# Layer 2's int8 feed-forward: whole numbers in bfloat16, scales at the result, bias and sum by GpSimd

## The chip, the cores and the metric

One core of a Trainium2 chip runs the whole program. The metric is the time of one execution on the device in microseconds, as the median of a few runs. Five engines work side by side, each in the order of its own queue: TensorE (PE in the profile, its weight loads PEld), VectorE (DVE), ScalarE (ACT), GpSimd (POOL) and SyncE (SP), which only issues transfers here. They hand work to each other through semaphores. [...]

## The reference, cut to what matters

A stream `x` of 4 x 256 tokens with 256 features goes through four layers. Each layer adds an attention and a feed-forward to the stream, both of the normalised stream and both under a gate, a tanh of one number:

```python
x = x + jnp.tanh(g_xattn[1]) * _L1_xattn_ref(_layernorm(x, axis=-1), ctx_512, ...)
x = x + jnp.tanh(g_ffn[1])   * _L1_ffn_ref(_layernorm(x, axis=-1), ...)      # ternary weights
x = x + jnp.tanh(g_xattn[2]) * _L2_xattn_ref(_layernorm(x, axis=-1), ctx_512, ...)
x = x + jnp.tanh(g_ffn[2])   * _L2_ffn_ref(_layernorm(x, axis=-1), ...)      # the changed stage
x = x + jnp.tanh(g_xattn[3]) * _L3_xattn_ref(...)
```

Layers 0 and 3 have a mixture of experts as feed-forward, layer 1 a two-layer network with ternary weights, layer 2 one matrix, quantised to 8 bits together with its input:

```python
def _L2_ffn_ref(x, weight, bias):
    w_max = jnp.clip(jnp.max(jnp.abs(weight), axis=1, keepdims=True), 1e-08, None)
    w_scale = w_max / 127
    w_q = jnp.clip(jnp.round(weight / w_scale), -128, 127).astype(jnp.int8)
    x_max = jnp.max(jnp.abs(x), axis=2, keepdims=True)
    x_scale = jnp.maximum(x_max / 127, 1e-12)
    x_q = jnp.clip(jnp.round(x / x_scale), -128, 127).astype(jnp.int8)
    acc = jnp.einsum('bnd,od->bno', x_q.astype(jnp.int32), w_q.astype(jnp.int32))
    y = acc.astype(jnp.float32) * x_scale * w_scale[None, None, :]
    return y + bias
```

`weight` is 256 x 256; each of its rows has a scale, and so has each token.

## The kernel before, in words

The tokens are cut into eight tiles of 128, `x[0]` to `x[7]`, which stay in SBUF all the time; four tiles make a group `g` of 512 tokens. The stages run one after the other: attention 0, the experts of layer 0, attention 1, layer 1's feed-forward, attention 2, the changed feed-forward (`ffn2`), attention 3, the experts of layer 3. The kernel is written as a dataflow, and a planner lays out each engine's queue at compile time: it goes through the program with a model of the durations, and when an engine is free it takes the earliest instruction of the program whose inputs are there. An instruction can thus be placed far ahead of its neighbours in the program, unless an edge holds it (`behind(later, sooner)`: not sooner than) or its tile has no buffer: tiles of one tag share a fixed number of buffers (`t4` six, `xn` six, `hits` one, the PSUM tag `mm` four).

Layer 2's weights are in the program in `weights2`, called ahead of layer 1's feed-forward. The weight lies as two halves `c` of 128 output rows. L1687 to L1690 find the scale `ws` of each row and its reciprocal; an edge keeps them behind attention 1's normalisation (`kept["normal"]`). L1695 to L1697 round (by adding and subtracting the constant ROUND), clip and multiply with the scale again, into a tile `wq` of the tag `t4`; L1698 multiplies with the gate. Four float32 transposes (L1704) and a copy by ScalarE (L1707) give `wqT`; the bias is one row of 1 KB (L1709), multiplied with the gate (L1710).

Around that time VectorE also makes layer 1's ternary weights (`ternary1`, L1608 and L1609, eight times each), and `ffn1` begins with transposes L1629 of its input's first group, which ScalarE and VectorE split into three bfloat16 terms (L1631 to L1634), for the products L1649 and the gelu L1656; L1665 is its second product, in bfloat16 with 256 columns.

In the changed stage, `rounded(g)` normalises a group (`layernorm`: statistics L382 and L383, root L385, reciprocal L386, shift L390, the normalised tiles L394 by ScalarE into four tiles of the tag `xn`), finds each token's largest value (L1719), and rounds by L1723 and L1724, the second of which multiplies with the token's scale again. Group 0's rounding is already called in attention 2. `ffn2` transposes the tiles in float32 (L409) into `xT` (one copy by ScalarE, L140, one by VectorE, L142); then for each tile TensorE lays down the bias (L1735, a product of one row of ones with one row of bias), adds two products (L1737), and VectorE adds the result to `x[t]` (L1740). Attention 3 begins with the normalisation of group 0 and its queries (L424).

Other lines that are spoken of: L440 is GpSimd's multiplication of the attention weights of one tile, L438 and L439 the sums and reciprocals ahead of it, L459 the addition of an attention's result to `x[t]`, L659 and L986 an attention's last products. L686 (VectorE) and L694, L695 (GpSimd) are attention 0's rotation of the queries. In layer 0's expert blocks GpSimd issues for each of 55 blocks a gather of its tokens (L1206) and a scatter of its result (L1305); at the end the sums are loaded back and added (L1488). L1320 and L1323 are VectorE's preparation of the last three blocks. L1602 and L1603 are two small steps of the ternary weights, L1030 and L871 memsets that belong to later stages.

Of the kernel before, what the change touches and what calls it, by code (L numbers as in the profile page):

```python
# [30 lines left out]
F32 = mybir.dt.float32  # L31
# [8 lines left out]
P = 128  # L40
# [48 lines left out]
def tile_flamingo(ctx: ExitStack, tc: tile.TileContext, a: dict, out: bass.AP):  # L89
# [1301 lines left out]
    def ffn0(gate):  # L1391
# [112 lines left out]
        )  # L1504
        moe.run(SURE0, collect)
        kept["fold1"] = ended[0]
        load_experts3(0, EARLY3, added[-1])

    def ffn3(gate):
# [169 lines left out]
        load_experts3(EARLY3, E3)  # L1679


    def weights2(gate):

        w = loaded["L2"][:, 1536:2048].rearrange("p (c d) -> p c d", c=2)
        ws = small([P, 2], "ws", 1)
        inv = small([P, 2], "wsi", 1)
        largest = nc.vector.tensor_reduce(ws, w, AX.X, ALU.max, apply_absolute_value=True)  # L1687
        behind(largest, kept["normal"])
        nc.vector.tensor_scalar(ws, ws, 1e-8, 1.0 / 127.0, ALU.max, ALU.mult)
        nc.vector.reciprocal(inv, ws)  # L1690
        wq = t4([P, 2, D], "wq")
        for c in range(2):

            q = wq[:, c, :]
            nc.vector.tensor_scalar(q, w[:, c, :], inv[:, c : c + 1], ROUND, ALU.mult, ALU.add)  # L1695
            nc.vector.tensor_scalar(q, q, ROUND, 127.0, ALU.subtract, ALU.min)
            nc.vector.tensor_scalar(q, q, -128.0, ws[:, c : c + 1], ALU.max, ALU.mult)  # L1697
        nc.vector.tensor_scalar(wq, wq, gate, None, ALU.mult)  # L1698
        kept_2 = sb.tile([P, 768], F32, tag="hits", name="kept_2", bufs=1)
        wqT = kept_2[:, :512].rearrange("p (d o) -> p d o", d=2)  # L1700
        ps = ps_mm()
        for d in range(2):
            for c in range(2):
                nc.tensor.transpose(  # L1704
                    ps[:, d * D + c * P : d * D + (c + 1) * P], wq[:, c, d * P : (d + 1) * P], ident
                )
        nc.scalar.copy(wqT.rearrange("p d o -> p (d o)"), ps)  # L1707
        bias_2 = kept_2[:1, 512:]
        nc.sync.dma_start(out=bias_2, in_=a["L2_bias"].partition_broadcast(1))  # L1709
        nc.vector.tensor_scalar(bias_2, bias_2, gate[:1], None, ALU.mult)  # L1710
        return wqT, bias_2

    def rounded(g):

        xn = layernorm(g, True)
        xs = small([P, TPG], "xs")
        xi = small([P, TPG], "xi")
        for i, n in enumerate(xn):
            nc.vector.tensor_reduce(xs[:, i : i + 1], n, AX.X, ALU.max, apply_absolute_value=True)  # L1719
        nc.vector.tensor_scalar(xs, xs, 1.0 / 127.0, 1e-12, ALU.mult, ALU.max)  # L1720
        nc.vector.reciprocal(xi, xs)
        for i, n in enumerate(xn):
            nc.vector.tensor_scalar(n, n, xi[:, i : i + 1], ROUND, ALU.mult, ALU.add)  # L1723
            nc.vector.tensor_scalar(n, n, ROUND, xs[:, i : i + 1], ALU.subtract, ALU.mult)  # L1724
        return xn

    def ffn2(gate):
        used("L2")
        wqT, bias_2 = kept.pop("weights2")
        for g in range(NG):  # L1730
            xqT = transposed(kept.pop("rounded") if g == 0 else rounded(g))
            for i in range(TPG):
                t = g * TPG + i
                ps = ps_mm()
                nc.tensor.matmul(ps[:, :D], ones[:1], bias_2, start=True, stop=False)  # L1735
                for d in range(2):
                    nc.tensor.matmul(  # L1737
                        ps[:, :D], xqT[:, d, i * P : (i + 1) * P], wqT[:, d, :], start=False, stop=(d == 1)
                    )
                nc.vector.tensor_tensor(x[t], ps[:, :D], x[t], ALU.add)  # L1740

    steps = [
        attention0,
# [159 lines left out]
```

## Time and profile before

| | |
|---|---|
| median of 3 runs | 934.46 us (933.23 to 937.22) |
| the profiled execution | 937.0 us, of which the span from first to last instruction 934.9 |
| TensorE busy | 850.5 us, 91% of the span |
| VectorE busy | 515.8 us, 55% |
| GpSimd busy | 317.9 us, 34% |
| ScalarE busy | 286.1 us, 31% |
| mean granted TensorE clock | 0.963 |
| attention 1 and ternary weights | 457 to 564 us |
| layer 1's feed-forward | 564 to 612 us |
| attention 2 | 612 to 677 us |
| the changed stage | 677 to 700 us |

A group in the profile is named by line, engine, operation, tile written from tile read, and shape; "idle before" is how long its engine stood still ahead of it and what ended that. The chain that ended last is followed back from the program's last instruction, at each step to what released it; what isn't on it has slack. A line of the chain in order of time gives the start, the duration and the engine, tile and line. TensorE takes a float32 product in two passes that are recorded one by one, so a float32 matmul counts twice among its instructions.

### The profile page before, as it was taken

What the parts mean: (1) busy time and instruction counts of PE and PEld (TensorE: products, weight loads), DVE (VectorE), ACT (ScalarE), POOL (GpSimd) and SP (SyncE); (2) the same over time, 40 slices, a digit from 0 to 9 for tenths busy, and PEclk for the clock granted to TensorE, in tenths of its full rate; (3) what the DMA queues carried; (4) which work ended last, traced back from release to release, by engine and by line L of the source; (5) the groups of instructions that cost most, each with busy time, mean ns of one, the idle gap of its engine ahead of it and who ended that gap; (6) DMA issues with size and microseconds to landing.
All of it is one profiled execution on the core that took longest, in us unless ns stands there. A gap on an engine that the chain in (4) does not pass through costs nothing.

```text
span 934.9 us, 12575 instructions
## 1 busy us (share of the span) xinstructions
PE 850.5 (91%) x4395; PEld 544.5 (58%) x4395; DVE 515.8 (55%) x1319; ACT 286.1 (31%) x545; POOL 317.9 (34%) x248
## 2 busy tenths in 40 slices
PE   5999998999978999899599978999889899999993
PEld 3544335875746777576446864755555556566662
DVE  3667446755843435333466787968767864222220
ACT  1221103434212332223133428526535531122220
POOL 0445442320027888887102220003202402244321
PEclk8999999999989999999899999989889999999997
DMA  9410218101684554555740000450000012122222
GB/s 343 139 35 6 96 48 270 48 23 28 215 248 82 87 87 80 85 83 80 219 159 1 1 1 1 143 200 1 1 23 1 1 47 64 46 47 46 35 23 63
DMA packets 38481, 74.90 MB, mean 80 GB/s; under 512 B 6225, under 2 KB 26290, under 8 KB 37042
## 3 DMA queue, kind: packets, MB, share of 16 engines
q1 hardware_dynamic: 24050, 53.34, 16.7%
q0 software_dynamic: 14016, 19.94, 13.4%
q8 instruction: 39, 0.64, 0.3%
q10 hardware_dynamic: 352, 0.79, 0.2%
q14 instruction: 24, 0.20, 0.1%
HBM read 58.87 MB, written 16.22 MB: 80 GB/s over the span
## 4 chain that ended last, share of the span: by engine, by line
PE 74%; DVE 9%; DMA 8%; ACT 4%; issue 2%; POOL 2%; SPq 0%; another core or an unknown queue 0%; POOLq 0%; ACTq 0%; DVEq 0%
PE wide L424 14%; PE wide L1264 8%; PE mm L1290 7%; PE wide L1253 6%; PE mm L424 5%; PE mm L659 4%; DMA xs<-xd,big 2%; PE wide L644 2%; PE mm L1665 2%; PE mm L454 2%; PE mm L1649 2%; PE mm L1280 2%; DMA sums<-ring,big 2%; PE wide L944 2%; PE mm L709 2%
## 5 line engine op out<-in xcount | busy, mean ns | idle before, releaser
L440 POOL TENSOR_TENSOR attn<-attn,sm 128x1024 f32<-128x1024 f32 x32 | 60.8, 1901 | 281.9 <-DVE sm L439 228.5
L1273 DVE SCALAR_TENSOR_TENSOR blk<-wide,blk 128x176 f32<-128x176 f32 (+1 forms) x75 | 37.0, 494 | 148.0 <-ACT blk L1272 141.0
L424 PE MATMUL wide<-xT,big 128*128 128x512 f32 (+1 forms) x240 | 111.3, 611 | 0.3 <-ACT xT L140 0.2
L1305 POOL DMA_INDIRECT sums<-ring,big x52 | 82.7, 1590 | 18.7 <-issue 7.8
L686 DVE TENSOR_TENSOR rope<-wide,big 128x512 f32<-128x512 f32 x96 | 59.6, 684 | 50.1 <-PE wide L424 50.1
L1253 PE MATMUL wide<-big,blk 128*128 x220 | 79.2, 478 | 3.3 <-issue 1.6
L1206 POOL DMA_INDIRECT xs<-xd,big x55 | 56.1, 1019 | 67.0 <-PE mm L581 43.1
L424 PEld LDWEIGHTS wide<-xT,big 128*128 128x128 f32 (+1 forms) x240 | 44.1, 192 | 57.1 <-issue 49.8
L1264 PE MATMUL wide<-big,blk 128*128 x160 | 74.3, 606 | 2.6 <-DMA sums<-x 2.2
L1272 ACT ACTIVATE blk<-wide 128x176 f32<-128x176 f32 (+1 forms) x75 | 29.4, 392 | 137.5 <-PE wide L1264 69.0
L1290 PE MATMUL mm<-big,blk 88*128 x220 | 58.2, 385 | 2.8 <-ACT blk L1282 2.1
L659 PE MATMUL mm<-vo,attnT 128*128 128x256 f32 x256 | 58.6, 382 | 1.5 <-ACT attnT L455 1.5
L1290 PEld LDWEIGHTS mm<-big,blk 88*128 88x128 f32 x220 | 42.0, 193 | 19.4 <-ACT blk L1282 3.8
L659 PEld LDWEIGHTS mm<-vo,attnT 128*128 128x128 f32 x256 | 47.4, 190 | 9.0 <-ACT attnT L455 3.2
L1253 PEld LDWEIGHTS wide<-big,blk 128*128 128x128 f32 x220 | 40.6, 197 | 18.6 <-issue 6.1
L455 ACT COPY attnT<-mm 128x512 f32<-128x512 f32 x64 | 34.6, 588 | 53.6 <-PE mm L454 53.2
L1264 PEld LDWEIGHTS wide<-big,blk 128*128 128x128 f32 x160 | 29.3, 194 | 33.3 <-issue 33.3
L438 DVE TENSOR_REDUCE sm<-attn 128x16 f32<-128x1024 f32 x32 | 38.9, 1215 | 16.2 <-ACT attn L432 13.7
L1305 POOL DMA_INDIRECT sums<-ring,scratch x20 | 31.5, 1573 | 41.0 <-ACT ring L1301 17.0
L1206 POOL DMA_INDIRECT xs<-xd,scratch x20 | 19.4, 972 | 73.5 <-PE mm L1218 49.7
L1219 DVE COPY blk<-mm 128x256 f32<-128x256 f32 x75 | 31.4, 419 | 17.0 <-PE mm L1218 14.4
L454 PE MATMUL mm<-ident,attn 128*128 128x128 f32 x256 | 35.1, 282 | 6.2 <-POOL attn L440 6.1
(311 smaller groups left out, 1607.2 us busy)
## 6 DMA issues: line engine op xcount, KB each, us to landing
big<-in_L_w_gate_up SPq DMA_DIRECT2D x8, 1024.0 KB, 8.9
big<-in_L_w SPq DMA_DIRECT2D x3, 1408.0 KB, 8.1
big<-in_L_w_down SPq DMA_DIRECT2D x8, 512.0 KB, 6.1
w_L_qk<-in_L_qk SPq DMA_DIRECT2D x4, 896.0 KB
big<-in_L_w SPq DMA_DIRECT2D x3, 768.0 KB, 7.1
big<-in_L_wo SPq DMA_DIRECT2D x1, 2048.0 KB, 13.0
xd<-xn SPq DMA_DIRECT2D x16, 128.0 KB, 1.8
w_L_wq<-in_L_wq SPq DMA_DIRECT2D x2, 1024.0 KB, 4.8
```

What stands on the lines that cost most here:

```text
L424: nc.tensor.matmul(ps, w(c), xT[:, c, :], start=(c == 0), stop=(c == 1))
L438: nc.vector.tensor_reduce(sm, e, AX.X, ALU.add)
L440: nc.gpsimd.tensor_tensor(e, e, sm.unsqueeze(2).to_broadcast([P, groups, n]), ALU.mult)
L454: nc.tensor.transpose(ps[:, i * P : (i + 1) * P], ev[:, pr * P : (pr + 1) * P], ident)
L659: nc.tensor.matmul(ps[:, :D], aT[:, s, :], vo[:, s, :], start=(s == 0), stop=(s == NP - 1))
L686: nc.vector.tensor_tensor(m[:, s, :].rearrange("q (b t) -> q b t", t=S), ps[:, s, :].rearrange("q (b t) -> q b t", t=S), table, ALU.mult,)
L1206: nc.gpsimd.indirect_dma_start(out=xs, out_offset=None, in_=self.xd, in_offset=bass.IndirectOffsetOnAxis(ap=self.gather[:, b : b + 1].bitc ...
L1253: nc.tensor.matmul(ps[:, 0, : 2 * n], st[:, c * P : (c + 1) * P], self.w[:, bass.ds(r + c * 2 * n, 2 * n)], start=False, stop=(c == 1),)
L1264: nc.tensor.matmul(ps[:, k, :n], st[:, c * P : (c + 1) * P], self.w[:, bass.ds(r + (2 * c + k) * n, n)], start=(c == 0), stop=(c == 1),)
L1273: self.weighted = nc.vector.scalar_tensor_tensor(s, lin, self.weight.pop(b), s, ALU.mult, ALU.mult)
L1290: nc.tensor.matmul(ps[:, :D], hT[:k, j * P : (j + 1) * P], self.w[:k, bass.ds(r + j * D, D)], start=(j == 0), stop=(j == self.n - 1),)
L1305: nc.gpsimd.indirect_dma_start(out=self.sums[b % len(self.sums)], out_offset=bass.IndirectOffsetOnAxis(ap=self.scatter[:, b : b + 1].bitca ...
```

## The change

The weights' quantisation is taken out of `weights2` into a new function `quantised`, which is called at the end of `ffn0`, with no edge to anything. It rounds and clips in place in the loaded weights, and leaves the whole numbers as bfloat16 in the first half of each 128 words; the scale isn't multiplied in. `weights2` transposes them in bfloat16, loads the bias into all 128 partitions and has GpSimd multiply it with the gate; it also makes a tile `scale`, each column's weight scale times the gate, in all partitions, by a product of ones with the scales on a diagonal (`spread`).

`rounded` no longer multiplies with the token's scale; its second step writes bfloat16 in place. GpSimd adds the bias to the group's `x[t]` there. `ffn2` transposes in bfloat16, has both copies made by ScalarE, and multiplies bfloat16 by bfloat16 with two products for a tile and none for the bias. VectorE then takes the result out of PSUM, times the token's scale and the column's scale, into a tile `y` of the tag `xn`, and GpSimd adds `y` to `x[t]`.

```diff
@@ -1504,6 +1504,7 @@
         )
         moe.run(SURE0, collect)
         kept["fold1"] = ended[0]
+        kept["quantised"] = quantised()
         load_experts3(0, EARLY3, added[-1])
 
     def ffn3(gate):
@@ -1679,39 +1680,48 @@
         load_experts3(EARLY3, E3)
 
 
-    def weights2(gate):
+    def quantised():
 
         w = loaded["L2"][:, 1536:2048].rearrange("p (c d) -> p c d", c=2)
+        q16 = loaded["L2"][:, 1536:2048].bitcast(BF16).rearrange("p (c d q) -> p c d q", c=2, d=2)[:, :, :, :P]
         ws = small([P, 2], "ws", 1)
         inv = small([P, 2], "wsi", 1)
-        largest = nc.vector.tensor_reduce(ws, w, AX.X, ALU.max, apply_absolute_value=True)
-        behind(largest, kept["normal"])
+        nc.vector.tensor_reduce(ws, w, AX.X, ALU.max, apply_absolute_value=True)
         nc.vector.tensor_scalar(ws, ws, 1e-8, 1.0 / 127.0, ALU.max, ALU.mult)
         nc.vector.reciprocal(inv, ws)
-        wq = t4([P, 2, D], "wq")
         for c in range(2):
-
-            q = wq[:, c, :]
-            nc.vector.tensor_scalar(q, w[:, c, :], inv[:, c : c + 1], ROUND, ALU.mult, ALU.add)
+            q = w[:, c, :]
+            nc.vector.tensor_scalar(q, q, inv[:, c : c + 1], ROUND, ALU.mult, ALU.add)
             nc.vector.tensor_scalar(q, q, ROUND, 127.0, ALU.subtract, ALU.min)
-            nc.vector.tensor_scalar(q, q, -128.0, ws[:, c : c + 1], ALU.max, ALU.mult)
-        nc.vector.tensor_scalar(wq, wq, gate, None, ALU.mult)
+            nc.vector.tensor_scalar(q16[:, c], q.rearrange("p (d q) -> p d q", d=2), -128.0, None, ALU.max)
+        return q16, ws
+
+    def weights2(gate):
+
+        q16, ws = kept.pop("quantised")
         kept_2 = sb.tile([P, 768], F32, tag="hits", name="kept_2", bufs=1)
-        wqT = kept_2[:, :512].rearrange("p (d o) -> p d o", d=2)
+        wqT = kept_2[:, :256].bitcast(BF16).rearrange("p (d o) -> p d o", d=2)
+        scale, bias = kept_2[:, 256:512], kept_2[:, 512:]
         ps = ps_mm()
+        flat = ps[:, :256].bitcast(BF16)
         for d in range(2):
             for c in range(2):
-                nc.tensor.transpose(
-                    ps[:, d * D + c * P : d * D + (c + 1) * P], wq[:, c, d * P : (d + 1) * P], ident
-                )
-        nc.scalar.copy(wqT.rearrange("p d o -> p (d o)"), ps)
-        bias_2 = kept_2[:1, 512:]
-        nc.sync.dma_start(out=bias_2, in_=a["L2_bias"].partition_broadcast(1))
-        nc.vector.tensor_scalar(bias_2, bias_2, gate[:1], None, ALU.mult)
-        return wqT, bias_2
+                nc.tensor.transpose(flat[:, d * D + c * P : d * D + (c + 1) * P], q16[:, c, d, :], ident16)
+        nc.scalar.copy(wqT.rearrange("p d o -> p (d o)"), flat)
+        nc.sync.dma_start(out=bias, in_=a["L2_bias"].partition_broadcast(P))
+        nc.gpsimd.tensor_scalar(bias, bias, gate, None, ALU.mult)
+        nc.vector.tensor_scalar(ws, ws, gate, None, ALU.mult)
+        spread = sb.tile([P, D], F32, tag="xn", name="spread", bufs=6)
+        for c in range(2):
+            nc.vector.tensor_scalar(spread[:, c * P : (c + 1) * P], ident, ws[:, c : c + 1], None, ALU.mult)
+        ps = ps_mm()
+        nc.tensor.matmul(ps[:, :D], ones, spread, start=True, stop=True)
+        nc.scalar.copy(scale, ps[:, :D])
+        return wqT, scale, bias
 
     def rounded(g):
 
+        bias = kept["weights2"][2]
         xn = layernorm(g, True)
         xs = small([P, TPG], "xs")
         xi = small([P, TPG], "xi")
@@ -1719,25 +1729,38 @@
             nc.vector.tensor_reduce(xs[:, i : i + 1], n, AX.X, ALU.max, apply_absolute_value=True)
         nc.vector.tensor_scalar(xs, xs, 1.0 / 127.0, 1e-12, ALU.mult, ALU.max)
         nc.vector.reciprocal(xi, xs)
+        whole_numbers = []
         for i, n in enumerate(xn):
             nc.vector.tensor_scalar(n, n, xi[:, i : i + 1], ROUND, ALU.mult, ALU.add)
-            nc.vector.tensor_scalar(n, n, ROUND, xs[:, i : i + 1], ALU.subtract, ALU.mult)
-        return xn
+            q = n.bitcast(BF16).rearrange("p (d q) -> p d q", d=2)[:, :, :P]
+            nc.vector.tensor_scalar(q, n.rearrange("p (d q) -> p d q", d=2), ROUND, None, ALU.subtract)
+            whole_numbers.append(q)
+        for i in range(TPG):
+            t = g * TPG + i
+            nc.gpsimd.tensor_tensor(x[t], x[t], bias, ALU.add)
+        return whole_numbers, xs
 
     def ffn2(gate):
         used("L2")
-        wqT, bias_2 = kept.pop("weights2")
+        wqT, scale, _ = kept["weights2"]
         for g in range(NG):
-            xqT = transposed(kept.pop("rounded") if g == 0 else rounded(g))
+            xq, xs = kept.pop("rounded") if g == 0 else rounded(g)
+            xqT = sb.tile([P, 2, TH], BF16, tag="xT", name="xT", bufs=2)
+            for c in range(2):
+                ps = ps_mm()[:, : TH // 2].bitcast(BF16)
+                for i, q in enumerate(xq):
+                    nc.tensor.transpose(ps[:, i * P : (i + 1) * P], q[:, c, :], ident16)
+                nc.scalar.copy(xqT[:, c, :], ps)
             for i in range(TPG):
                 t = g * TPG + i
                 ps = ps_mm()
-                nc.tensor.matmul(ps[:, :D], ones[:1], bias_2, start=True, stop=False)
                 for d in range(2):
                     nc.tensor.matmul(
-                        ps[:, :D], xqT[:, d, i * P : (i + 1) * P], wqT[:, d, :], start=False, stop=(d == 1)
+                        ps[:, :D], xqT[:, d, i * P : (i + 1) * P], wqT[:, d, :], start=(d == 0), stop=(d == 1)
                     )
-                nc.vector.tensor_tensor(x[t], ps[:, :D], x[t], ALU.add)
+                y = sb.tile([P, D], F32, tag="xn", name="y", bufs=6)
+                nc.vector.scalar_tensor_tensor(y, ps[:, :D], xs[:, i : i + 1], scale, ALU.mult, ALU.mult)
+                nc.gpsimd.tensor_tensor(x[t], x[t], y, ALU.add)
 
     steps = [
         attention0,
```

## The prediction

> **What bounds the kernel now.** I read the page's fourth part first (TensorE has 74% of the chain that ended last, VectorE 9%, GpSimd 2%), then a table of busy time by stage, then that chain in order of time at the two places where the code changes. In the table the columns are the stretch, its length, and busy microseconds of PE, PEld, DVE, ACT and POOL, then the granted clock and the DMA share.
>
> ```profile
> 278.00:450.00 172.00, 162.94 (x739) 119.05 (x740) 67.04 (x257) 49.35 (x139) 132.96 (x101) 0.97 0.52 85
> ...
> 557.00:562.00 5.00, 0.00 (x0) 0.00 (x0) 5.00 (x14) 0.00 (x0) 0.00 (x0) 0.99 0.00 0
> ...
> 580.00:590.00 10.00, 10.00 (x48) 4.55 (x47) 9.93 (x10) 9.94 (x14) 0.00 (x0) 1.00 0.00 0
> ...
> 688.00:694.00 6.00, 5.75 (x16) 3.77 (x16) 2.04 (x7) 2.66 (x5) 0.00 (x0) 0.52 0.01 3
> ```
>
> In layer 0's expert blocks (278 to 450) GpSimd is busy 133 us in 101 instructions, and nearly every one stands 0.30 us behind the one before: 133 + 101 x 0.30 = 163 of 172 us. GpSimd is full there, VectorE is 39% busy. From 557 to 562 only VectorE works. From 572 on, layer 1's feed-forward has TensorE, VectorE and ScalarE full together, so what is gained ahead of it comes through as a shift, and nothing more is gained in it. From 688 to 694, in the changed stage, TensorE has half its clock.
>
> The chain where layer 2's weights are quantised (start, duration, what):
>
> ```profile
> 555.99 0.26 DVE wq L1695
> ...
> 561.67 0.41 DVE wq L1698
> 562.08 0.04 issue
> 562.12 1.12 PE mm L1704 x4
> 563.24 1.72 PE mm L1629 x8
> ...
> 571.09 0.70 ACT h L1656
> ```
>
> The weights' reciprocal was done at 478.1, yet L1695 starts at 555.9: its buffer `wq` is one of the six `t4` that attention 1 turns over, and they are handed out in the order of the program. So it falls between the ternary weights' steps (L1608, L1609), and the transposes L1704 wait for it with L1629, layer 1's first transposes, queued behind them; TensorE stands still for 5.21 us.
>
> The chain in the stage itself:
>
> ```profile
> 677.96 1.05 PE mm L1735 x4
> 679.01 1.92 PE mm L1737 x8
> ...
> 684.35 0.42 DVE x L1740
> ...
> 690.45 0.59 ACT xT L140
> 691.04 0.04 issue
> 691.09 3.78 PE mm L1737 x8
> ...
> 699.46 3.70 PE mm L424 x8
> ```
>
> [...]On the chain between 677 and 699.5 the products L1737 have 9.95 us and the bias rows L1735 5.41 us; between the two groups of tiles it goes over VectorE's rounding. At 699.46 layer 3's queries begin. No run but this profile is behind the durations: its time is 937.0 us, 934.9 of it the span; the median of the runs is 934.46. I add up a difference and take it from the median.
>
> **The weights' rounding leaves 555.9 to 563.** Off the chain: L1695, L1696, L1697 twice each and L1698, 0.26+0.21+0.26+0.26+0.20+0.26+0.41 = 1.86 us, and L1704's 1.12. The new transposes need neither `wq` nor the rounding at that time, so they can run when attention 1's last products are done (556.9), and L1629 after them. Then VectorE is next: the last ternary step ends 1.86 earlier, and the waits behind it for ScalarE's copies (0.90 before L1632, 0.58 before L1634) close because the copies are made meanwhile. 1.86 + 0.90 + 0.58 = 3.3; a part of the 1.12 comes on top. Lower bound of the gain 1.9 (the rows alone), upper 5.21 + 1.12 = 6.3 (all of TensorE's wait). I take **-3.6**, near VectorE's sum, since VectorE is the engine without a gap here.
>
> **Where the rounding goes.** It has no order against anything but the weights' load (issued at 272.9, landed 10.2 us later) and no shared buffer. The planner takes work when its inputs are there: layer 3's memset L1030 of `scratch` runs at 666, in layer 2's attention. So I expect it among the blocks, early. It is one reduction (0.68), two small steps (0.17 each) and six on 256 columns (0.35+0.29, and 0.35 for the one that writes bfloat16; rows L1695 to L1697). VectorE has room; GpSimd hasn't. Rows of the timeline:
>
> ```profile
> 354.05 2.00 POOL L1206 DMA_INDIRECT xs<-xd,big  x1 [0.30 <-DVE at L1320]
> ...
> 547.56 1.90 POOL L440 TENSOR_TENSOR attn<-attn,sm 128x1024 f32<-128x1024 f32 x1 [0.70 <-DVE sm L439]
> 547.62 0.15 DVE L1602 TENSOR_SCALAR thr<-mm 128x2 f32<-128x2 f32 x1
> ...
> 548.08 3.19 DVE L1603 TENSOR_SCALAR nthr<-thr 128x2 f32<-128x2 f32 x1
> ```
>
> The gather L1206 takes 0.99 by the median and 2.00 under VectorE's 1.22 us L1323, which reads two arrays; and L1603, the same two columns as L1602 but out of SBUF instead of PSUM, stood 3.19 until GpSimd had finished. [...] By the rows the price is GpSimd's: 2 x (0.35+0.29+0.35) = 1.98, times GpSimd's share of time 0.8, **+1.6**. Bounds: 0 (placed at 444 to 457, where VectorE waits 14.4 us for loads) and 2.7 (everything, the reduction too).
>
> **What stays in weights2.** Four bfloat16 transposes, at most L1704's 1.12; a float32 product for the scales, 0.48 (half of four L1735 records is 0.53); ScalarE 0.59 and 0.37 (L983); VectorE two steps on 128 columns and a small one, under 0.9; GpSimd's bias step, 0.7 at most. They fill gaps in attention 1: **+0.3**, at worst 1.5, since the chain there is TensorE's. The bias load grows from 1 to 128 KB. SP held L1709 2.75 us; the next on SP is at 590, so nobody waits. It queues behind experts 0 to 3 (6 MB), and GpSimd's step waits for it, with attention 1's L440 behind. GpSimd idles 43.15 us before its first L440 at 492.9 and the DMA engines are quiet from 482: ten microseconds of cover; past them, each one costs one.
>
> **The stage itself.** The bfloat16 product on 256 columns is L1665's: 20.97/192 = 0.109 against 0.48 to 0.53 for L1737. Sixteen of them are 1.7 us. Bfloat16 transposes have no row: between half of 0.109 and L409's 0.87/8 = 0.11; I take 0.06. GpSimd's sum on 256 columns lies between L440 on 128 (0.401) and L694 on 512 (1.272): 0.69, against L1740's 0.42 on VectorE, and sixteen of them are 11.0. L1740's place is taken by a form like L459, 0.48. Both copies of the transposed input are now ScalarE's, 2 x 0.59 in a row.
>
> Group 0: L986 ends 677.1; transposes 0.5, copies to 678.7, first result 679.0, evacuated 679.5, GpSimd's four sums to 682.3; before, 684.8. Group 1: its inputs are ready from attention, ScalarE writes them 682.0 to 684.1 as now, GpSimd's bias sums run to 685.4 beside VectorE's reductions, and may hold L1720; so the rounding ends as now, 688.3. Transposes and copies to 689.8 (before 691.0), results evacuated from 690.3, sums to 693.6. Layer 3's first normalised tiles share six `xn` buffers with the new `y`: two start at once, the others when GpSimd has read the first two `y`, 691.5 and 692.2, and end 693.3. Transposes, a copy: queries at 694.8 for 699.46, -4.7. Against it stands the clock. Row: eight L1737 records take 1.92 warm and 3.78 at clock 0.52. [...] I take 0.7: **-4.0**. Bounds: -7 (the queries before group 1) and +3.
>
> **Sum:** -3.6 + 1.6 + 0.3 - 4.0 = -5.7; 937.0 becomes 931.3, the median 934.46 becomes **928.8**. All after it is TensorE's chain to the end and moves along.
>
> **Rivals.** *The waits go whole* (0.22): nothing paid in the blocks, 6.3 and 5 us won: 923.2. For it: the 14.4 us gap at the blocks' end. Against: VectorE's ternary steps don't get shorter. *The change doesn't do what it says* (0.15): the scales' product or its copy takes wq's place in the queue ahead of L1629 (its buffers too are handed out in order), so only 1.9 is won, the blocks take 1.6 back, and the stage gives 1: 933.5. [...]
>
> **From cases to numbers.** Half a per cent, 4.7 us, is about what a measurement of this kernel tells from no change. The sum above has 0.47, with its own range 925.5 to 932: 0.37 under 929.8 and 0.10 within. Faster 0.37 + 0.22 = 0.59; same 0.10 + 0.15 = 0.25; slower 0.16. The range 922.5 to 938 leaves out half of the slow case and the tails.
>
> **What would show it.** Right: no `wq` on the chain, L1629 before 560, layer 1's first gelu near 567.5 (less what the blocks add), the blocks' last scatter 1 to 2 us later, queries of layer 3 some 4 us nearer to the end of layer 2's attention. Wrong: a VectorE tensor_scalar of 1 us or more in the stage, GpSimd's first L440 late, L1206 and L1305 unchanged in sum, or the rounding at 444 to 457.

## The result and the profile after

The changed kernel takes 942.68 us (median of 13 runs, 937.68 to 948.62); the kernel before, run beside it, takes 935.64 (13 runs, 932.76 to 941.83). The ratio is 1.0065, with a 95% interval of 1.0039 to 1.0091: about 6 us slower. 928.8 was forecast, with a range up to 938. The profiled execution took 945.44 us, 943.5 of them the span, at a mean granted clock of 0.949 (937.0, 934.9 and 0.963 before).

Line numbers of the changed kernel, where they differ: the rounding of the weights is L1689 to L1696, the scales' gate L1713, their product L1718, layer 1's transposes and products L1630 and L1650, the ternary steps L1604, L1609 and L1610, the stage's products L1758, its results L1762 and sums L1740 and L1763.

**The blocks begin 11 us later.** The timeline of the changed kernel where layer 0's expert blocks begin (start, duration, engine, line, what; in brackets the idle time before and what ended it):

```profile
273.08 1.21 SPq L227 DMA_DIRECT2D w_L<-in_L_weight  x1
...
275.96 0.96 POOL L1206 DMA_INDIRECT xs<-xd,big  x1 [0.30 <-issue]
283.29 0.69 DVE L1689 TENSOR_REDUCE ws<-w_L 128x2 f32<-128x512 f32 x1 [9.68 <-DMA w_L<-in_L_weight]
284.01 0.17 DVE L1690 TENSOR_SCALAR ws<-ws 128x2 f32<-128x2 f32 x1
284.21 0.17 DVE L1691 RECIPROCAL wsi<-ws 128x2 f32<-128x2 f32 x1
...
285.77 1.09 PE L1218 MATMUL mm<-ident,xs 128*128 128x128 f32 x4 [12.69 <-DVEq L1351]
...
288.93 2.68 PE L1253 MATMUL wide<-big,blk 128*128 x4 [1.56 <-DVE w_L L1696]
```

The same place in the kernel before:

```profile
273.96 0.23 DVE L1230 SCALAR_TENSOR_TENSOR own<-fixed,big,xs 128x16 f32<-128x16 f32 x1 [1.56 <-DVEq L1351]
...
277.98 2.68 PE L1253 MATMUL wide<-big,blk 128*128 x4 [1.13 <-DMA w_L_w<-in_L_w]
```

L1351 is the branch into the blocks that are needed only sometimes; in the trace each engine has its own branch instruction there, ScalarE and GpSimd at 272.2, SyncE at 275.8, VectorE at 285.3. The planner put the first three steps of the rounding ahead of VectorE's. The weights' load, issued at 273.08, landed at 283.3, so VectorE stood for 9.68 us ahead of the branch, and TensorE, whose first product behind it (L1218) waited for VectorE's branch, for 12.69. The first product of the blocks moved from 277.98 to 288.93.

**The junction gains less than forecast.** The chain between attention 1 and layer 1's feed-forward, in order of time (start, duration, what):

```profile
562.20 0.50 DVE low L1609
562.70 0.03 issue
562.72 0.76 DVE w_L_w L1610
563.48 0.03 issue
...
571.47 0.61 DVE more L1633
...
574.94 1.86 PE mm L1650 x4
...
579.56 6.85 PE mm L1650 x31
```

There is no `wq`, and the first four L1630 begin 0.55 us after attention 1's last product, with the weights' transposes and the scale's product between, as forecast. But the other four wait 2.50 us more, until VectorE has done L459, an addition that stands among the ternary steps. The ternary steps follow each other without a break to 572.7. And the first four L1650 of the chain take 1.86 us, where the four L1649 of before took 1.02: TensorE has half its clock there (0.50 from 572 to 577 in the table below). From the step `nthr` to the main run of products, the stretch that is called the junction from here on, it was 548.08 to 571.83, 23.75 us; it is 557.66 to 579.56, 21.90.

**The stage gains what was forecast, and pays more for the clock.** From the timeline of the changed stage:

```profile
682.35 1.13 PE L986 MATMUL mm<-w_L,ctxTok 128*128 128x256 f32 x4 [0.55 <-ACT ctxTok L983]
...
686.41 2.77 POOL L1763 TENSOR_TENSOR x<-x,y 128x256 f32<-128x256 f32 x4 [4.63 <-DVE y L1762]
...
691.16 0.76 DVE L390 SCALAR_TENSOR_TENSOR shift<-mv,rstd 128x4 f32<-128x4 f32 x1
...
692.92 0.70 PE L1752 MATMUL mm<-ident,xn 128*128 128x128 bf16 x4 [6.74 <-DVE xn L1736]
...
697.48 1.29 ACT L394 ACTIVATE xn<-x,shift,rstd 128x256 f32<-128x256 f32 x2 [1.05 <-POOL x L1763]
...
701.03 5.23 PE L424 MATMUL mm<-xT,w_L 128*128 128x512 f32 x8 [1.52 <-ACT xT L140]
```

The queries L424 begin 18.68 us after attention 2's last product began, where it was 23.51 (675.95 to 699.46): 4.8 us less. They take 5.23 us for the 3.70 of before.

**And attention 3 loses 5 us more in this execution.** Busy time by stage (stretch, length, busy time of PE, PEld, DVE, ACT and POOL, granted clock, DMA share):

```profile
289.00:459.00 170.00, 161.71 (x739) 117.68 (x740) 66.05 (x255) 49.34 (x139) 130.62 (x100) 0.98 0.49 80
...
572.00:577.00 5.00, 3.55 (x10) 1.18 (x9) 4.30 (x11) 2.76 (x4) 0.00 (x0) 0.50 0.00 0
...
683.00:688.00 5.00, 2.40 (x19) 1.23 (x17) 4.23 (x16) 2.72 (x5) 1.59 (x3) 0.91 0.32 105
688.00:694.00 6.00, 0.86 (x6) 0.47 (x6) 5.72 (x23) 2.30 (x5) 3.90 (x6) 0.50 0.00 1
...
700.00:706.00 6.00, 4.97 (x8) 2.09 (x8) 1.00 (x5) 3.35 (x7) 0.00 (x0) 0.65 0.01 3
...
717.00:728.00 11.00, 11.00 (x51) 6.66 (x50) 5.59 (x9) 3.19 (x6) 3.00 (x2) 0.54 0.00 0
```

The blocks themselves are as they were. From 717 to 728 TensorE is busy throughout, nearly all of it at half clock (0.54). Summed over the marks, against before: +9.6 at `nthr`, -1.85 in the junction, -1.3 in attention 2 (at its end the clock stood at half for 6.83 us in the profile of before, from 667.75, and for 3.41 in this one, from 673.42), -3.2 from attention 2's last product to layer 3's second queries, +5.4 from there to the end: +8.6, the difference of the two spans.

### The profile page after: what moved, and what is told of

It is laid out like the page before. It is cut to its first block, busy times and chain, and to the rows that moved or that the text cites. A ratio compares the mean times of both kernels' runs of the same rounds, so it can differ in the third digit from the quotient of the medians.

```text
span 943.5 us, 12538 instructions
## 1 busy us (share of the span) xinstructions
PE 844.0 (89%) x4362; PEld 539.3 (57%) x4365; DVE 514.6 (55%) x1318; ACT 287.6 (30%) x548; POOL 329.0 (35%) x265
## 4 chain that ended last, share of the span: by engine, by line
PE 50%; DVE 8%; DMA 4%; ACT 3%; issue 2%; POOL 1%; POOLq 0%; DVEq 0%; ACTq 0%; SPq 0%
PE mm L1290 7%; PE wide L1264 7%; PE wide L1253 6%; PE mm L424 4%; PE wide L424 3%; DMA xs<-xd,big 3%; PE mm L1280 2%; PE mm L1666 2%; PE mm L1650 2%; PE wide L944 2%; PE mm L454 2%; PE mm L1542 1%; PE mm L659 1%; PE mm L986 1%; PE wide L644 1%
## 5 line engine op out<-in xcount | busy, mean ns | idle before, releaser
L440 POOL TENSOR_TENSOR attn<-attn,sm 128x1024 f32<-128x1024 f32 x32 | 60.8, 1901 | 226.0 <-DVE sm L439 191.5
L424 PE MATMUL wide<-xT,big 128*128 128x512 f32 (+1 forms) x240 | 110.7, 608 | 0.6 <-ACT big L559 0.3
L1206 POOL DMA_INDIRECT xs<-xd,big x55 | 56.1, 1019 | 74.5 <-PE mm L581 43.0
L1253 PE MATMUL wide<-big,blk 128*128 x220 | 78.1, 473 | 3.9 <-issue 2.3
L424 PEld LDWEIGHTS wide<-xT,big 128*128 128x128 f32 (+1 forms) x240 | 43.9, 191 | 57.0 <-issue 49.2
L1264 PE MATMUL wide<-big,blk 128*128 x160 | 72.6, 595 | 2.8 <-DMA sums<-x 2.3
L1253 PEld LDWEIGHTS wide<-big,blk 128*128 128x128 f32 x220 | 40.2, 195 | 18.6 <-issue 5.6
L1218 PE MATMUL mm<-ident,xs 128*128 128x128 f32 x150 | 29.4, 280 | 14.3 <-DVEq L1351 12.7
L454 PE MATMUL mm<-ident,attn 128*128 128x128 f32 x256 | 35.5, 284 | 6.4 <-POOL attn L440 6.3
```

The costliest lines, as they stand in the source:

```text
L424: nc.tensor.matmul(ps, w(c), xT[:, c, :], start=(c == 0), stop=(c == 1))
L440: nc.gpsimd.tensor_tensor(e, e, sm.unsqueeze(2).to_broadcast([P, groups, n]), ALU.mult)
L454: nc.tensor.transpose(ps[:, i * P : (i + 1) * P], ev[:, pr * P : (pr + 1) * P], ident)
L1206: nc.gpsimd.indirect_dma_start(out=xs, out_offset=None, in_=self.xd, in_offset=bass.IndirectOffsetOnAxis(ap=self.gather[:, b : b + 1].bitc ...
L1253: nc.tensor.matmul(ps[:, 0, : 2 * n], st[:, c * P : (c + 1) * P], self.w[:, bass.ds(r + c * 2 * n, 2 * n)], start=False, stop=(c == 1),)
L1264: nc.tensor.matmul(ps[:, k, :n], st[:, c * P : (c + 1) * P], self.w[:, bass.ds(r + (2 * c + k) * n, n)], start=(c == 0), stop=(c == 1),)
```

## The experiments

Theory 1: the wait for the weights' load ahead of the branch is what the change lost. Theory 2: the moved steps themselves are, beside GpSimd's work in the blocks, and only the forecast's 1.6 us come back when they leave it. Theory 3: the half clock in attention 3 is. A further question was how the gains in junction and stage divide. The kernel before took 938 to 939 us beside these runs, so ratios to it are what is compared.

### The rounding held back to the gap

```diff
-                nc.vector.tensor_copy(y, ps[:, :D])
+                kept["copied"] = nc.vector.tensor_copy(y, ps[:, :D])
...
+            kept["quantised"] = quantised()
             for t in range(0, NT, 2):
...
+            for done in added:
+                behind(done, kept["rounding"])
...
-        nc.vector.tensor_reduce(ws, w, AX.X, ALU.max, apply_absolute_value=True)
+        largest = nc.vector.tensor_reduce(ws, w, AX.X, ALU.max, apply_absolute_value=True)
+        behind(largest, kept["copied"])
```

> The changed kernel, with one difference: the rounding of layer 2's weights is held behind the last of VectorE's copies in the expert blocks, so that it stands in the gap in which VectorE waits for the partial sums. Theory 1 (VectorE's wait for the weights' load ahead of the branch into the blocks is what the change lost): the first L1253 is back near 278, the last scatter of the blocks near 448, and the time falls by 8.5 to 10 us, from 942.7 to about 933.5. [...] Theory 3 (all of the loss is the half clock in layer 3's attention): nothing comes back at the blocks' start: 942 or 943.

Measured: ratio 0.9961 (0.9938 to 0.9984), 935.64 us. From 1.0065 that is 1.04%, some 9.7 us. In the timeline of this run the steps stand where VectorE used to wait 14.4 us for the sums, and the first L1253 is at 276.96:

```profile
439.67 0.42 DVE L1299 COPY ring<-mm 128x256 f32<-128x256 f32 x1
440.01 0.68 DVE L1691 TENSOR_REDUCE ws<-w_L 128x2 f32<-128x512 f32 x1
...
442.06 0.70 DVE L1699 TENSOR_SCALAR w_L<-w_L 128x256 bf16<-128x256 f32 x2
...
456.36 2.49 DVE L1489 TENSOR_TENSOR x<-x,more 128x512 f32<-128x512 f32 x4 [13.60 <-DMA more<-sums]
```

Theory 1 holds, and theories 2 and 3 fall as the main cause: the same work, held back to that gap, costs nothing that can be seen.

### The wait without the change

```diff
-        largest = nc.vector.tensor_reduce(ws, w, AX.X, ALU.max, apply_absolute_value=True)
-        behind(largest, kept["normal"])
+        nc.vector.tensor_reduce(ws, w, AX.X, ALU.max, apply_absolute_value=True)
```

> The kernel before, with one line less: the reduction over layer 2's weights has no order any more behind layer 2's normalised input, so that it can stand ahead of the branch into the expert blocks. Everything else is as before: float32 products, rounding by wq in attention 1. Theory 1 (the wait): the blocks start 9 to 11 us later, and 8.5 to 10 of it reach the end: 944 to 945.5 for 935.6. [...] Theory 3 (half clock in layer 3's attention): the stage is the old one, so no loss: 935.6.

Measured: ratio 1.0073 (1.0047 to 1.01), 945.36 us, with the old rounding and the old stage. In its timeline:

```profile
284.02 0.69 DVE L1687 TENSOR_REDUCE ws<-w_L 128x2 f32<-128x512 f32 x1 [10.55 <-DMA w_L<-in_L_weight]
...
289.57 2.68 PE L1253 MATMUL wide<-big,blk 128*128 x4 [1.60 <-issue]
```

Three small steps, moved ahead of the branch, cost as much as the whole change lost. By the median 6.9 us, less than the 8.5 to 10 expected, though the interval (4.4 to 9.4) reaches into it; the span of its profile was 11.8 us longer.

### The move alone

```diff
-    def weights2(gate):
+    def quantised(gate):
...
-        behind(largest, kept["normal"])
+        behind(largest, kept["copied"])
...
-        wq = t4([P, 2, D], "wq")
...
-        nc.vector.tensor_scalar(wq, wq, gate, None, ALU.mult)
+        kept["rounding"] = nc.vector.tensor_scalar(w, w, gate, None, ALU.mult)
+        return w
```

> The kernel before, with the rounding of layer 2's weights alone moved, in float32 and in place, into the gap in which VectorE waits for the partial sums at the end of the expert blocks; scales, gate, bias, products and sums as before. It prices the junction by itself. By the prediction's step (3.6 us for wq's seven steps and the waits behind them): 932. By the trace of the changed kernel (the pairs of ternary steps lose 0.25 us each that the interleaved steps used to fill, and layer 1's first products run at half clock after TensorE's wait): a gain of 1.9 or less, 933.7 or more. If the steps cost something in the gap, more than 935.6.

Measured: ratio 0.9993 (0.9974 to 1.0013). The prediction's 3.6 us would be 0.996 and lie outside this interval; a gain of 1.85 us and no gain at all both lie inside. From `nthr` to the main run it is 549.34 to 571.24, 21.90 us, to the hundredth what the changed kernel has: by the profile the junction is worth 1.85 as it stands, whatever the form of the stage. The rest of the gain of the run before (0.3% between the two, with intervals that overlap) is the stage's; its own stretch is 30.57 us here, 30.50 before and 27.48 there.

### TensorE kept at work in the stage

```diff
+            if g == 0:
+                spare = ps_mm()
+                for _ in range(22):
+                    nc.tensor.matmul(spare.rearrange("p (h l) -> p h l", l=L), ident16,
+                                     causal16.unsqueeze(1).to_broadcast([P, 8, L]), start=True, stop=True)
```

> As the run with the rounding in the gap, and 22 bfloat16 products of 128 by 512 that nobody reads follow the first group's products in layer 2's feed-forward, where TensorE stands idle for 6.7 us; they add work and no result. Theory of the clock (TensorE's idle time in the stage brings it to half clock in layer 3's queries and again in layer 3's attention): the granted clock stays at 1.00 from 683 on, eight L424 take 3.70 instead of 5.23, and the time falls by 1.5 to 6.5 us against the run with the rounding in the gap alone, to about 929. If the clock in layer 3's attention falls for another reason (a wait of its own): 1.5 at most, 932. If the extra products only stand in the way: 933.5 or more.

Measured: ratio 0.9951 (0.9928 to 0.9973), not told apart from 0.9961, and L424 takes 5.40 still. The table by stage shows why (same columns):

```profile
682.00:684.00 2.00, 1.93 (x9) 0.68 (x7) 1.94 (x10) 1.02 (x3) 2.00 (x4) 1.00 0.02 4
684.00:686.00 2.00, 0.35 (x4) 0.23 (x4) 1.97 (x8) 0.00 (x0) 0.63 (x1) 1.00 0.00 0
686.00:688.00 2.00, 0.93 (x8) 0.48 (x7) 0.73 (x4) 0.95 (x2) 0.00 (x0) 0.89 0.00 0
688.00:690.00 2.00, 2.00 (x11) 1.23 (x10) 1.23 (x4) 1.10 (x3) 0.61 (x1) 0.50 0.00 0
...
692.00:694.00 2.00, 0.30 (x1) 0.30 (x2) 1.49 (x7) 0.97 (x3) 0.17 (x1) 1.00 0.00 0
694.00:696.00 2.00, 2.00 (x4) 0.76 (x3) 0.00 (x0) 1.87 (x4) 0.00 (x0) 0.60 0.00 0
```

The products keep the clock up to 687. It falls after the next gap (684 to 688), comes back, and falls again just as the queries begin, after the gap at 692. The expectation took one gap for the cause; each gap is one of its own.

### The sums on VectorE

```diff
-            nc.gpsimd.tensor_tensor(x[t], x[t], bias, ALU.add)
+            nc.vector.tensor_tensor(x[t], x[t], bias, ALU.add)
...
-                nc.gpsimd.tensor_tensor(x[t], x[t], y, ALU.add)
+                nc.vector.tensor_tensor(x[t], x[t], y, ALU.add)
```

> The changed kernel with the rounding in the gap, and the stage's sixteen sums on 256 columns (bias and result) given back to VectorE; the rest as in the run with the rounding in the gap, whose ratio to the kernel before was 0.9961. Theory of the prediction's sum (GpSimd's sums lie beside VectorE's work and take it off the chain): VectorE is busy without a gap from 677.5 to 684.1 there, eight of the sums at 0.42 us now fall into or ahead of that stretch, and the layer 3 queries come 2 to 3.5 us later: ratio 0.998 to 1.000. [...]

Measured: ratio 0.9934 (0.9912 to 0.9957), which overlaps with 0.9961. The queries begin 18.13 us after attention 2's last product (18.68 with GpSimd), the second ones 27.14 (27.48). The 2 to 3.5 us of the expectation did not come: without GpSimd's sums beside them L390 falls from 0.76 to 0.14 and L1733 from 0.32 to 0.16, and layer 3's second pair of tiles waits 0.15 for its sum and not 1.05, but group 1's rounding is reached 0.8 us later. The two effects cancel, as far as one profile shows: with the sums on GpSimd the second queries come 27.05 to 27.48 us after that product in five profiles.

### Clock and a buffer for y

Edit, on top of the rounding in the gap; `keep_busy(n)` is n of the products above:

```diff
+            ys = t4([P, TPG, D], "ys")
...
-                y = sb.tile([P, D], F32, tag="xn", name="y", bufs=6)
+                y = ys[:, i, :]
...
+            keep_busy(26 if g == 0 else 5)
...
+            if layer == 3 and g == 0:
+                keep_busy(8)
...
+                if g == 0:
+                    keep_busy(8 if c == 0 else 2)
...
+                            if g == 0 and f == 0 and k == 1:
+                                keep_busy(5)
```

> The changed kernel with the rounding in the gap, with two additions: the results y have a buffer of their own (they shared the six of xn), and bfloat16 products that nobody reads fill TensorE's idle time at four places: behind layer 1's first transposes and in its first products (20), behind each group of layer 2's products (26 and 5), and behind the first transposes of layer 3's queries (8). They add work and no result. Theory of the clock: the products of layer 1 that stood at half clock (0.43 apart) stand 0.22 apart, 1.1 us sooner from the ternary threshold to the second products (40.0 before, 38.9 or less now); eight L424 of layer 3 take 3.70 instead of 5.40, 1.7 sooner. Theory of the shared buffer: the second pair of layer 3's normalised tiles no longer waits 1.05 us for GpSimd, about 1 us sooner. Together 3.8: 18.7 us from layer 2's last attention product to the queries become 17.7, and the ratio to the kernel before 0.992. If the clock has no part in it, 0.995.

Measured: ratio 0.9916 (0.9888 to 0.9943). In the stage both parts came: eight L424 (here L435) take 3.60, and the second queries come 24.85 us after attention 2's last product, 2.6 less. The junction gained nothing, 22.07 us: its products stand 0.22 apart, at full clock, but the eight products behind the first transposes waited for a PSUM tile until VectorE had read attention 1's last result, with the second transposes behind them:

```profile
558.92 1.89 PE L106 MATMUL mm<-causal,ident 128*128 128x512 bf16 x8 [2.50 <-DVE x L470]
...
560.64 0.60 PE L1645 MATMUL mm<-ident,xn 128*128 128x128 f32 x4
```

### The changed kernel once more

> The changed kernel once more, unaltered, beside the others on this chip, with a second profile. If the 10 us at half clock in layer 3's attention (the first profile lost 5 us there) belong to the change, they are in this profile too, and the shift between layer 3's queries and the end grows from about 3 to 8 us again. If they belong to that execution alone, this profile has no half clock there, its time is nearer to 940, and what is left of the loss is the wait ahead of the branch less what junction and stage give: ratio 1.005 to 1.0075.

Measured: ratio 1.0037 (1.0016 to 1.0058), by its middle under the 1.005 to 1.0075 that were expected, and a profile with a span of 936.1 us. From its timeline and its table by stage:

```profile
574.00 0.38 PE L1650 MATMUL mm<-xT,w_L_w 128*128 128x512 bf16 x1 [1.16 <-ACT xT L1634]
574.22 0.38 PE L1650 MATMUL mm<-more,w_L_w 128*128 128x512 bf16 x1
574.44 0.38 PE L1650 MATMUL mm<-xT,w_L_w 128*128 128x512 bf16 x1
```

```profile
717.00:728.00 11.00, 11.00 (x91) 6.52 (x82) 9.58 (x15) 5.27 (x10) 2.82 (x2) 1.00 0.01 1
```

The half clock from 717 to 728 is absent, so theory 3's 5 us belong to single executions, not to the change. The junction's last products, from 574.00 on, happened to run at full clock (0.22 apart, 0.43 in the first profile); the half clock of this one (0.70 from 570 to 575) lies ahead of them, and behind it TensorE waits 1.16 us for ScalarE, as it does in the first profile. `nthr` to the main run is 20.80 us, so the clock of those products is worth 1.1, and the junction with them at full clock 2.95. (The other profiles with the moved rounding and without filling products all have 21.90.) The blocks begin at 288.48: the wait is in both profiles.

### The same with the best parts

Edit against the run for clock and buffer: none of the filling products behind the first transposes, five behind the second, three behind the first term.

```diff
-                if g == 0:
-                    keep_busy(8 if c == 0 else 2)
+                if g == 0 and c == 1:
+                    keep_busy(5)
...
-                            if g == 0 and f == 0 and k == 1:
-                                keep_busy(5)
+                            if g == 0 and f == 0 and k == 1 and c == 0:
+                                keep_busy(3)
```

> As the run for the clock and the own y (rounding in the gap, y in a buffer of its own, TensorE kept at work by products that nobody reads), with fewer of these products in layer 1's first products: none behind the first group of transposes, where the last run's eight waited for a PSUM tile and held the second group back by 1.7 us, five behind the second, three behind the first term. Clock theory: the ternary threshold to the main run of products falls from 22.07 to 20.8, which the second profile of the changed kernel showed at full clock; ratio to the kernel before 0.990. If those products wait for anything else, 22 again and 0.9915.

Measured: ratio 0.9897 (0.9863 to 0.9931), 929.54 us. The junction takes 20.80, as the clock theory had it, and TensorE has its full clock in it (the products stand 0.22 apart); the stage takes 25.37 to the second queries. Run again later beside another kernel:

> The twin with the sums on GpSimd once more, unaltered, beside the other on the same chip, for the comparison and as the best version: 25.4 us from layer 2's last attention product to layer 3's second queries, ratio to the kernel before 0.988 to 0.992.

Measured: 0.9897 again (0.9863 to 0.9932), 928.35 us, with 20.80 and 25.40. This version beats both kernels: by 1.0% the one before, and by about 1.5% the changed one.

Its twin has the sixteen sums on VectorE, by the same edit as above:

> The same as the other run of this call that keeps TensorE at work, and one difference: the sixteen sums of the stage by VectorE instead of GpSimd. [...] The traces of the two runs so far (queries 18.7 and 18.1 us after layer 2's last attention product) point to agreement within 1 us.

Measured: ratio 0.9947 (0.9923 to 0.997), and 29.47 us in the stage. Not the sums did that, but the order: in this version the planner put the second group's results ahead of layer 3's first shift.

```profile
686.82 0.75 DVE L1784 TENSOR_TENSOR x<-x,ys 128x256 f32<-128x256 f32 x2
687.48 0.16 DVE L401 SCALAR_TENSOR_TENSOR shift<-mv,rstd 128x4 f32<-128x4 f32 x1
687.68 2.08 ACT L405 ACTIVATE xn<-x,shift,rstd 128x256 f32<-128x256 f32 x4 [3.28 <-DVE shift L401]
```

With one edge that puts them behind it:

```diff
+            for scaled in kept.pop("scaled", ()):
+                behind(scaled, shifted)
```

> As the run with the sums on VectorE and TensorE kept at work, and one more edge: the second group's four scalings y stand behind layer 3's first shift L401 on VectorE. In that run they stood ahead of it and held layer 3's first normalised tiles back by 3 us. If that order was all that made it slower than its twin with the sums on GpSimd (29.5 against 25.4 us from layer 2's last attention product to layer 3's second queries), this one needs 25 to 25.5 and its time agrees with the twin's within 0.2%: GpSimd's part of the change is worth nothing here. If GpSimd's sums are worth something by themselves, it needs 27 or more.

Measured: ratio 0.9915 (0.9886 to 0.9944), 929.83 us, and 25.99 us in the stage, half a microsecond over what was expected. So the order cost 3.5 us in the stage. GpSimd's part of the change is worth 0.6 us there by the two profiles (25.40 against 25.99); the two times agree within 0.2%, which is less than their intervals tell apart. In both twins with the sums on VectorE the eight products in layer 1 did not keep the clock: the junction's products stood 0.43 apart for some 3 us (559.4 to 562.4 in the first twin), and it took 21.14 and 21.15.

### The load first

```diff
+            if quant:
+                nc.sync.dma_start(out=w[:, 1536:2048].rearrange("p (c d) -> p c d", c=2),
+                                  in_=a["L2_weight"].rearrange("(c p) d -> p c d", p=P))
             nc.sync.dma_start(out=w[:, :1024], in_=a[f"L{layer}_q_out"])
```

> The changed kernel with the rounding where the planner put it, ahead of the branch, and the load of layer 2's weights issued as the first of the three loads of its tile instead of the last, about 1 us sooner on SP. Nine VectorE steps (2.6 us) now stand ahead of the branch, where three did. Theory of the wait: the blocks begin when the load has landed and these steps are done, wherever the load comes in the queue; if it lands by 1 to 3 us sooner, start and end are 0 to 2 us sooner or later than in the changed kernel, in step with the landing, and the time stays above the kernel before: ratio 1.003 to 1.008. If the position ahead of the branch and not the load is what costs, the blocks start 2.6 us later than before plus what stood there, whatever the landing: ratio under 1.001.

Measured: ratio 1.0003 (0.9981 to 1.0026), below the 1.003 to 1.008 of the theory of the wait. Its timeline:

```profile
281.10 0.69 DVE L1689 TENSOR_REDUCE ws<-w_L 128x2 f32<-128x512 f32 x1 [7.60 <-DMA w_L<-in_L_weight]
...
287.73 2.69 PE L1253 MATMUL wide<-big,blk 128*128 x4 [1.59 <-issue]
```

The landing is 2.2 us sooner and the wait 2.1 shorter, with all nine steps (and the scales' gate) ahead of the branch now; the blocks begin 0.8 to 1.2 us sooner than in the two profiles of the changed kernel. That far it goes with the landing, and the start expected by the other theory, 2.6 us later than before, is far off. But `nthr` comes at 554.00, 2.7 and 3.7 us sooner than there. So some 2 us more came back than the wait explains, as if the six steps inside the first blocks had cost that. Two other causes are on record: `nthr` itself lies between 546.24 and 550.58 in the ten profiles without the wait, and TensorE's half clock after the wait reached 2.9 us into the blocks here, 5.6 and 4.6 in the two profiles of the changed kernel. No run separates the three, and it stays open.

## Why the prediction was wrong

**Where the rounding goes: the step that failed.** The prediction said that the rounding "has no order against anything but the weights' load (issued at 272.9, landed 10.2 us later)", expected it "among the blocks, early", and had it in the sum at +1.6 for GpSimd, with bounds of 0 and 2.7. Issue and landing were known; what was not asked is what stands behind an instruction that waits for them. A queue is fixed when the program is built: once the planner has put the reduction ahead of the branch, VectorE waits for the load (9.68 us), and what needs VectorE behind the branch waits with it: TensorE's products 12.69 us, GpSimd's next gather 9.84. This term was +9.6 and +8.6 at `nthr` in the two profiles, and 0.5 less each against the mean of the ten profiles without the wait (548.6). The rounding in the gap gave the time back and the wait alone made it, so this is shown. No run shows the 1.6 us, which were an estimate: the gathers of the blocks sum to 56.1 us before and after, the scatters to 82.7 before and 82.0 after. The prediction had named just that, sums that don't change, as a sign of being wrong.

**The weights' rounding leaves 555.9 to 563.** Forecast -3.6 (bounds -1.9 to -6.3); measured -1.85, and -2.95 where the junction's last products ran at full clock. The mechanism was right, two sizes were off. VectorE's seven steps were counted at 1.86, but a ternary pair (L1608 and L1609) takes 1.31 us by itself and took 1.53 with two of them in between:

```profile
555.59 0.39 DVE low L1608
555.99 0.26 DVE wq L1695
556.25 0.66 DVE w_L_w L1609
556.91 0.21 DVE wq L1696
557.12 0.40 DVE low L1608
```

So the two added 0.22 us and not the 0.47 that they have on the chain. The seven were worth 0.9: from `nthr` to the end of the last ternary step 0.3 us went, and L1633 (0.61) now lies inside. The rest of the 2.95, about 2, are the transposes and copies ahead of layer 1's products, where the prediction had 1.5 and a part of 1.1. And half clock, which the term did not have, took back 1.1.

**What stays in weights2.** Forecast +0.3. The bias step of GpSimd ran at 489.98, after a load of 13.1 us for which only GpSimd, idle there, waited; it took 0.93 us where 0.7 at most was forecast, and cost nothing. The transposes and the scale's product (0.39 and 0.65) lie between attention 1's end and L1630, inside the term: nothing to correct. With that, the rival in which the scale's product takes wq's place falls; that its 1.9 us is what the junction gave is luck.

**The stage itself.** Forecast -4.7 ahead of the clock, measured -4.8; its pieces (0.69 for a sum by GpSimd; the shared `xn` buffers that hold two of layer 3's tiles back, here by 1.05) came as described. The clock was taken at +0.7, a term that no run shows; it is +1.5 in the changed kernel (L424 x8 at 5.23 for 3.70), +1.7 with the rounding in the gap and with TensorE kept at work (5.40 each), and +2.2 with the sums on VectorE (5.93). Taking it that low was the error. TensorE waits 6.74 us ahead of L1752; the clock fell at 687.08, 0.9 us after TensorE's last product of group 0 (686.2), and came back at 704.14. With that wait filled but for 1.72 us, the queries still took 5.40; with the places around the second group and ahead of the queries filled too, 3.60. So filling TensorE's idle time in the stage gave the clock back, and filling that one wait did not. Net -3.2 for -4.0.

**The rivals.** *Slower* (0.16) had the right sign; it was set on GpSimd's sums in the stage, and the loss came ahead of the blocks. In the stage L1730, in both groups, and L390 paid about 1 us together (0.32, 0.17 and 0.61 over the 0.15 that they take alone), while the rounding steps began at 692.04, when GpSimd's bias sums were over (691.91). Giving the sums back to VectorE moved the second queries by -0.3 us in one pair of profiles and by +0.6 in the other. *The waits go whole* falls too: it had 6.3 us from the junction, which gave 2.95 at best. The sum with the measured sizes is about +8.6 - 2.4 - 3.2, some 3 us slower, and more in an execution with half clock in attention 3; the two measurements gave 6.1 and 3.5.

## What to carry to other kernels

An instruction that is moved to an earlier place takes its wait with it: look up when its input lands, and what stands behind it on its engine. A branch is such a place: here TensorE's first product behind it waited 12.69 us because of one load ahead of it on VectorE. If it has to be early, hold it with edges to a place where its engine waits anyway; here that was worth about 1%. What made the stage short for TensorE here also made it idle, and the half clock behind that took back 1.5 to 1.7 of the 4.8 us that were won: such a loss belongs into the sum in full.

## What the runs showed of the hardware

- Half clock came in whole steps of 3.41 us. In the clock records of the kernel before and of the changed kernel every stretch of half clock inside the program lasts 3.41 us or two to five times that, up to 17.07 (from 687.08 on in the changed kernel), and the stretches between them are whole multiples too. In the first profile of the changed kernel one of them is in attention 3, with TensorE busy from 718 on:

```profile
716.00:718.00 2.00, 1.30 (x10) 1.13 (x12) 2.00 (x4) 0.61 (x2) 1.54 (x2) 0.95 0.00 0
718.00:720.00 2.00, 2.00 (x14) 1.16 (x16) 0.10 (x1) 1.42 (x2) 1.01 (x1) 0.50 0.00 0
...
728.00:730.00 2.00, 2.00 (x24) 1.18 (x23) 0.23 (x1) 1.59 (x3) 0.80 (x1) 0.99 0.00 0
```

  A clock of 0.95 over 2 us is half clock for the last 0.2, and 0.99 for the first 0.04: it lasted from 717.80 to 728.04, 10.24 us or three steps.
- The same gap went with full clock in some profiles and with half clock in others. TensorE's longest gap in attention 3, ahead of a transpose L454 that waits for GpSimd's L440, takes 1.84 us in the changed kernel, 1.85 with the load first and 1.62 in the move alone, and there the clock fell, for 10.24, 10.24 and 6.83 us. It takes 1.63 in the kernel before, and 1.84 in the second profile of the changed kernel and with the rounding in the gap, and there the clock stood at 1.00 from 708 to 736. Laid over the steps that the clock's own changes mark, the gap lies whole inside one step in the three that fell (714.86 to 716.70 in the step from 714.39 to 717.80 in the changed kernel); the clock fell at the end of that step, in which TensorE was busy for 46 to 52%. In the kernel before the edge of a step cuts the gap (712.12 in 712.07 to 713.70), and with the rounding in the gap too (705.35 in 705.20 to 707.04). That this decides is not shown: in the wait alone a gap of about 1.6 us, by its clock record inside one step too, left the clock at 1.00 from 708 to 736.
- Work that nobody reads paid here: 39 bfloat16 products beside the chain (26 and 5 in the stage, 8 ahead of the queries) took L424 from 5.40 to 3.60; clock and own y, both runs of the best parts and the version with the order put right each show the 3.60. Eight in layer 1's first products, at their right place, went with full clock and 1.1 us less in two profiles (20.80 for 21.90), and in the two with the sums on VectorE they did not keep the clock (21.14 and 21.15); a few instructions sooner they waited 2.50 for a PSUM tile and took as much as they gave (22.07).
